# A three-level seven-for-eight product with its result transposed, in a kernel of layer norm, attention and a low-rank layer

## The chip, the cores and the metric

The kernel runs on one core of one Trainium2 chip. The metric is the time of one execution on the device in microseconds (us), median of three runs. A profile of one execution comes with it. The engines are named as the profile does: PE multiplies matrices and reads its weights through PEld, DVE, ACT and POOL compute on vectors, SP issues transfers (DMA). SBUF is the memory beside the engines, PSUM the one that PE writes its products to, in eight banks; DRAM is the memory outside.

## The reference

All values are 32-bit floats. `x` has the shape (4, 512, 1024): four batches of 512 tokens.

```python
xn = _layernorm(x, axis=-1)
qkv = hidden_states @ w_qkv                      # of xn: 32 heads of 128, 8 shared k and v heads
scores = jnp.einsum('bqhgd,bkhd->bhgqk', q, k) * scale
bias = -slopes[:, :, None, None] * sqrt_dist     # -inf above the diagonal
attn = jax.nn.softmax(scores + bias[None], axis=-1)
out = jnp.einsum('bhgqk,bkhd->bqhgd', attn, v).reshape(B, S, NH * D)
return out @ w_o
...
out = jnp.einsum('bsd,od->bso', hidden_states, W) + b      # of xn
lora_outputs = jnp.stack([x @ A[:r, :].T @ B[:, :r].T for r in RANKS], axis=1)
# one of the four ranks 8, 16, 32, 64 is chosen per token by a gate
...
x = x + _L0_attn_ref(xn, ...) + _L0_ffn_ref(xn, ...)
```

The two products that end in the result, `out @ w_o` over 4096 attention columns and `xn @ W.T` over 1024, have the same rows and columns. So the kernel computes one product: 2048 tokens by a contraction of 5120 by 1024 columns, and adds the low-rank term and `x`.

## The kernel before

**Seven products for eight.** A product of two matrices cut in quarters can be made with seven products of quarters. With the quarters a11 to a22 of the left matrix and b11 to b22 of the right one, `sums_a` (L142) forms s1 = a21 + a22, s2 = s1 - a11, s3 = a11 - a21, s4 = a12 - s2, and `sums_b` (L149) t1 = b12 - b11, t2 = b22 - t1, t3 = b22 - b12, t4 = b21 - t2. The products, by number, are a11·b11, a12·b21, s4·b22, a22·t4, s1·t1, s2·t2 and s3·t3 (`operand_a`, `operand_b`). The class `Inner` (L162) runs the seven in the order m1, m5, m4 of the item before, m6, m3, m2, m7, adds several into the same PSUM bank where it can, and has DVE or ACT read a bank out after each step: `read` (L173) by ACT if nothing is to be added to it and by DVE if there is, `last` (L182) always by DVE. A step's bank is used again by a step soon after, so a late read delays PE. A matmul of 32-bit floats is two instructions on PE.

**Stages.** PE's instructions keep the order of the program. On the other engines a scheduler sets the order, except where a call is wrapped in `pin`. The stages follow each other and overlap a little at their borders.

1. `project()` (L357) normalises `x`, transposes it and computes q, k and v with two levels of seven for eight: `sets` of columns for each pair p of batches, items i of the outer level in the order `PROJECTED`, and the seven inner steps of each by `Inner`. POOL makes the inner sums of the weights (`inner_w`, L504), DVE the outer ones (`outer_w`, L489) and the inner ones of the tokens (`Pair.inner`, L462). Work beside the steps stands in the queues `soon`, `later` and `weights`; `beside()` (L578) takes a piece of each after every step, of `later` only after every eighth (`pace[1]`). `put_by` (L443) stores the outer sums of the normalised tokens for the last product.
2. `attend()` (L765) runs over 32 units (p, h, bi): pair, shared head, batch in the pair. The scores of the next unit are made between the steps of the present one. For a row i of 128 tokens, PE makes four score tiles in three banks (L819), DVE adds the bias and finds the maximum (L824), ACT takes the exponential (L828), DVE inverts the sum (L831), POOL scales (L833), PE transposes (L844), DVE and ACT by turns copy the transposed tile to SBUF (`pt`, L847 and L849), PE multiplies with v (L857) and ACT copies the result into the tile `o` (L858). After the second batch of a head `put_by(p, h)` (L860) makes the four outer sums of the two batches' results on POOL (in `os`) and stores seven operands in 14 transfers of 256 KB on SP's queue; for the last head DVE makes the sums and ACT's queue takes the stores. `outer_weights()` (L875) goes on beside: 20 pieces of the weights are loaded, POOL makes four subtractions of 128 x 512 in each, and four sums are stored.
3. `finish()` (L1026) computes the last product with two levels: `order` (L950) has 2·7·2 = 28 items (p, i, kb): pair of batches, outer product, half of the contraction. `Operands` (L952) loads the four quarters of tokens (`sa`, L979) and of weights (`sw`, L971 to L976), 640 KB each. DVE makes the four token sums of an item and POOL the four weight sums, each on a tile of 128 x 1280 (`first_sums`, `sums`). A step is 5 x 2 matmuls with 128 tokens as PE's weights and 256 columns moving (L1016). The results of outer products stay in SBUF, in five tiles `r8` of 2048 values per partition, are summed there by `take_over` (POOL) and `after`, and leave from there (`store`, L1131). `x` comes in as the start value of each result quarter (`given`). The low-rank term is two more matmuls in four steps of four items (L1157).

Tokens' outer sums pass from stages 1 and 2 to stage 3 through DRAM (`s_d`), those of the weights from stage 2 (`t_d`). The tiles of the first item are loaded late in attention (`bring`), its first two sums are made there too (`add_up`), and its steps m1 and m5 are run among attention's last steps (`begin`, banks `begun`). These lines set it:

```python
order = [(p, i, kb) for p in range(NP) for i in OUTER for kb in range(2)]
...
for i in (3, 2, 1, 0):
    if nxt:
        scores(nxt, i)
    if i < 2:
        weigh(u, i + 2)
...
    transpose_probs(u, i)
...
weigh(u, 1)
...
weigh(u, 0)
...
if u[2] == 1:
    put_by(u[0], u[1])
```

Of the kernel before, what the change touches and what calls it, by code (L numbers as in the profile page):

```python
# [18 lines left out]
P = 128  # L19
# [34 lines left out]


@with_exitstack
def kernel(
# [35 lines left out]
    stats = ctx.enter_context(tc.tile_pool(name="stats", bufs=2))  # L93
# [19 lines left out]
    ag = const.tile([P, NC, RMAX + NR], F32, tag="ag", name="ag")  # L113
    gb = const.tile([P, NR], F32, tag="gb", name="gb")


    def scratch(name, shape):
# [7 lines left out]
    s_d = {  # L125
        (p, i, kb): scratch(f"s{p}_{i}_{kb}", [P, 2, 2, KB, HS])
        for p in range(NP) for i in OUTER for kb in range(2)
    }
    t_d = {(i, kb): scratch(f"t{i}_{kb}", [P, 2, 2, KB, HS]) for i in (4, 5, 6, 7) for kb in range(2)}

    def by_quarters(d, kp, src, queue=nc.sync):

        for e in range(2):
            queue.dma_start(out=d[:, :, e, kp, :], in_=src[:, e, :].rearrange("p (r k) -> p r k", r=2))
# [27 lines left out]
    class Inner:  # L162
# [10 lines left out]
        def read(self, dst, src, row, col):  # L173
            if self.base is None:
                if self.begun is None:
                    nc.scalar.copy(dst, src)  # L176
                else:
                    nc.vector.tensor_copy(dst, src)
            else:
                add(nc.vector, dst, src, self.base(row, col))  # L180
# [10 lines left out]
        def first(self, which, m):  # L191
            if self.begun is not None:
                return self.begun[which]
            bank = self.bank(which, self.name)
            self.mult(m, bank, True)
            return bank
# [20 lines left out]
        def m2(self):  # L217
            a = self.bank("a", self.name)
            self.mult(2, a, True)
            self.last(0, 0, a, self.t1)  # L220
# [65 lines left out]

    us = {}
# [69 lines left out]
    def project():  # L357
        with pool("a") as sb:
# [60 lines left out]
            class Pair:  # L419
# [3 lines left out]
                def __init__(self, p, homes):  # L423
                    self.p, self.homes, self.X, self.XO, self.XI = p, homes, {}, {}, {}
# [18 lines left out]
                def put_by(self, i):  # L443
                    for c in range(2):
                        by_quarters(s_d[self.p, i, 0], c, self.XO[i][:, c::2, :])
# [16 lines left out]
                def inner(self, i, eng):  # L462
# [4 lines left out]
                    t = buf(f"xi{i}", f"xi{i}_{self.p}")  # L467
# [185 lines left out]

            def once(f, *args):
# [7 lines left out]
            def hand_over(a, b, i):  # L662
# [15 lines left out]
                else:  # L678
                    soon.append(once(b.home, 3))
                    for j in (3, 7, 4, 5):  # L680
                        if j in (3, 7):
                            soon.append(b.outer(j, (V, V, V, V)))
                        soon.append(once(b.put_by, j))
                        soon.append(b.inner(j, V))
                    soon.extend(once(b.put_by, j) for j in (1, 2, 6))

            def stream():
# [28 lines left out]
                for st in sets[:2]:  # L716
                    for i in (1, 2):
                        need(a, i)
                        yield item(st, i, accs[st])
                        if st == sets[0] and i == 1:  # L720
                            for j in (1, 2):
                                soon.append(once(a.put_by, j))
# [9 lines left out]
                for j in (3, 7, 4, 5):  # L732
                    if j in (3, 7):
                        soon.append(a.outer(j, (V, V, V, V)))
                    soon.append(once(a.put_by, j))
                    soon.append(a.inner(j, GP if j == 4 else V))
                soon.append(once(a.put_by, 6))
# [27 lines left out]
    def attend(front, begin):  # L765


        with pool("b") as sb:
            bank = rotation(sc=(0, 1, 2), tr=(3, 6, 7), o=(4, 5))
            units = [(p, h, bi) for p in range(NP) for h in range(NKV) for bi in range(2)]  # L770
            sizes = {"wr": (2, DOUT), "wsum": (2, S), "q": (G, S), "k": (S,), "vT": (S,), "bias": (G, S)}
            counts = {"q": 2, "k": 2, "vT": 2, "v": 2, "pt": 10, "o": 3}
# [3 lines left out]
            sizes.update(v=(NT, D), pt=(S,), os=(3, 2, S), o=(G, S))  # L776
# [83 lines left out]
            def put_by(p, h):  # L860

                o = [O.pop((p, h, bi)) for bi in range(2)]
                a = [o[r][:, 2 * j : 2 * j + 2, :] for r in range(2) for j in range(2)]
                t = buf("os", f"os_{p}_{h}")
                s = [t[:, 0], t[:, 1], a[2], t[:, 2]]
                end = (p, h) == (NP - 1, NKV - 1)
                sums_a(nc.vector if end else nc.gpsimd, *s, *a)
                kb, kp = divmod(h + 2, KB)
                for i in OUTER:
                    by_quarters(  # L870
                        s_d[p, i, kb], kp, operand_a(i, a[0], a[1], a[3], s),
                        nc.scalar if end else nc.sync,
                    )

            def outer_weights():  # L875

                for kb in range(2):
                    for kp in range(KB):
                        for e in range(2):
                            n = f"{kb}_{kp}_{e}"  # L880
                            w = buf("wr", f"wr_{n}")
                            pin(nc.sync.dma_start(
                                out=w, in_=rows_of(kb * KB + kp, slice(0, DOUT))[:, :, e]
                            ))
                            yield
                            b11, b12, b21, b22 = [w[:, k, ts(j, S)] for k in range(2) for j in range(2)]
                            t = buf("wsum", f"wsum_{n}")
                            pin(sub(nc.gpsimd, t[:, 0], b12, b11))
                            pin(sub(nc.gpsimd, t[:, 1], b22, t[:, 0]))
                            pin(sub(nc.gpsimd, b12, b22, b12))  # L890
                            pin(sub(nc.gpsimd, b21, b21, t[:, 1]))
                            for i, v in ((5, t[:, 0]), (6, t[:, 1]), (7, b12), (4, b21)):
                                nc.sync.dma_start(
                                    out=t_d[i, kb][:, :, e, kp, :],
                                    in_=v.rearrange("p (r k) -> p r k", r=2),
                                )
                            yield
# [335 lines left out]
```

## Time and profile before

| | |
|---|---|
| median of 3 runs | 2765.87 us (2763.76 to 2769.19) |
| the profiled execution | 2767.64 us |
| its span | 2765.8 us |
| mean clock granted to PE | 0.989 of full speed |
| instructions | 34769 |
| transfers | 450.6 MB, 163 GB/s over the span |
| score tiles, L819 (PE) / L824 (DVE) | x1024, 441 ns / x512, 490 ns |
| exponentials L828 (ACT) / scalings L833 (POOL) | x512, 554 ns / x512, 537 ns |
| transposes L844 / products with v L857 (PE) | x1280, 275 ns / x640, 592 ns |
| `s<-o`, `s<-os` (stores of attention) | x120 and x90, 256 KB each, 2.8 and 2.6 us to landing |
| `sa<-s`, `sw<-t` (loads of the last product) | x112 and x64, 640 KB each, 6.2 and 4.1 us to landing |

The times are one execution's, by the hardware profiler. "x1024, 441 ns" is a count and the mean time of one. Tile names stand left and right of an arrow: what is written, from what is read. Matmuls overlap, so the time of one is longer than the distance to the next. The projections last until about 1132 us after the span's start, attention until about 1873 us, the last product until the end. Where rows of a stage are compared, they come from the stretches 50 to 900, 1190 to 1850 and 1850 to 2766 us.

### The profile page before, as it was taken

To read this page: it belongs to the slowest core of one execution; us is meant where nothing else is said; L and a number is where in the kernel's file an instruction comes from. 1 tells how busy PE (TensorE), PEld (TensorE's weight loads), DVE (VectorE), ACT (ScalarE), POOL (GpSimd) and SP (SyncE) were. 2 spreads that over 40 slices of the span, in tenths; PEclk is the share of its full clock that TensorE was granted. 3 is DMA by queue.
4 is the path that set the end of the run, shared out by engine and by line. 5 is a ranking of instruction groups with operands and counts; after the bars stand their busy time and mean duration, and the time that the engine had idled before them with its cause. 6 is when DMAs were issued, how large, how long until landed. Compare 5 with 4: busy or idle time off the path is not lost.

```text
span 2765.8 us, 34769 instructions
## 1 busy us (share of the span) xinstructions
PE 2687.0 (97%) x12224; PEld 2158.9 (78%) x12224; DVE 1417.7 (51%) x3093; ACT 628.4 (23%) x1671; POOL 1579.2 (57%) x1670
## 2 busy tenths in 40 slices
PE   7899999989999999899999999997999999999999
PEld 6788888878888888566666666656888888888887
DVE  7655656576565555455555555554333442334432
ACT  3011111000000000566666666650000000000000
POOL 4565656666766666468787775654435433534531
PEclk9999999999999999999999999998999999999999
DMA  6333332263223221457676764627566556656551
GB/s 225 118 115 122 119 119 98 103 232 111 92 100 114 92 99 54 143 193 261 223 257 225 255 229 160 221 88 253 176 196 201 170 195 201 189 177 190 175 185 40
DMA packets 250400, 450.59 MB, mean 163 GB/s; under 512 B 17193, under 2 KB 164649, under 8 KB 246130
## 3 DMA queue, kind: packets, MB, share of 16 engines
q1 hardware_dynamic: 245554, 441.55, 47.5%
q10 hardware_dynamic: 4672, 6.82, 0.7%
q8 instruction: 97, 1.59, 0.2%
q14 instruction: 77, 0.63, 0.1%
HBM read 290.49 MB, written 157.82 MB: 162 GB/s over the span
## 4 chain that ended last, share of the span: by engine, by line
PE 91%; DVE 6%; DMA 2%; issue 1%; ACT 0%; POOL 0%; ACTq 0%; DVEq 0%; POOLq 0%
PE pc L1016 17%; PE pc_q L525 13%; PE po L857 10%; PE psc L819 10%; PE pd L1016 8%; PE pd_q L525 7%; PE pc_kv L525 6%; PE pa L1016 4%; PE ptr L844 4%; PE pa_q L525 3%; PE pd_kv L525 3%; PE pa_kv L525 2%; DVE pt L847 1%; DVE p L824 1%; PE pc_begun L1016 1%
## 5 line engine op out<-in xcount | busy, mean ns | idle before, releaser
L833 POOL TENSOR_SCALAR p<-p,tot 128x256 f32<-128x256 f32 (+3 forms) x512 | 262.9, 537 | 161.0 <-DVE tot L831 120.6
L140 POOL TENSOR_TENSOR t<-sw,sw 128x1280 f32<-128x1280 f32 x28 | 82.1, 2931 | 448.9 <-DMA sw<-t 260.9
L824 DVE CUSTOM_DVE_ANT_0 p<-psc,bias 128x256 f32<-128x256 f32 (+3 forms) x512 | 243.5, 490 | 156.7 <-PE psc L819 109.2
L819 PE MATMUL psc<-k,q 128*128 128x512 f32 (+3 forms) x1024 | 309.9, 441 | 12.3 <-DMA q<-q 6.6
L828 ACT ACTIVATE p<-p,low 128x256 f32<-128x256 f32 (+3 forms) x512 | 283.4, 554 | 84.3 <-DVE low L824 80.8
L857 PE MATMUL po<-pt,v 128*128 128x512 f32 x640 | 290.6, 592 | 0.0
L819 PEld LDWEIGHTS psc<-k,q 128*128 128x128 f32 x1024 | 173.3, 192 | 115.3 <-issue 60.6
L1016 PE MATMUL pc<-sw,sa 128*128 128x256 f32 x1080 | 237.7, 379 | 0.0
L1016 PEld LDWEIGHTS pc<-sw,sa 128*128 128x128 f32 x1080 | 205.2, 190 | 27.9
L844 PEld LDWEIGHTS ptr<-ident,p 128*128 128x128 f32 x1280 | 148.4, 141 | 70.9 <-POOL p L833 26.1
L847 DVE COPY pt<-ptr 128x512 f32<-128x512 f32 x192 | 130.2, 684 | 139.7 <-PE ptr L844 139.3
L857 PEld LDWEIGHTS po<-pt,v 128*128 128x128 f32 x640 | 116.8, 190 | 108.5 <-issue 99.2
L525 PE MATMUL pc_q<-xi,ti_q 128*128 128x256 f32 x704 | 182.1, 381 | 3.7 <-DVE q L137 2.4
L140 POOL TENSOR_TENSOR ti_q<-to_q 128x256 f32<-128x256 f32 x128 | 97.7, 783 | 136.2 <-PE pc_q L525 136.2
L844 PE MATMUL ptr<-ident,p 128*128 128x128 f32 x1280 | 168.6, 275 | 4.1 <-DVE pt L847 2.7
L525 PE MATMUL pc_q<-x,ti_q 128*128 128x256 f32 x640 | 165.4, 381 | 3.8 <-DVE r_q L137 2.5
L140 POOL TENSOR_TENSOR t<-sw,t 128x1280 f32<-128x1280 f32 x56 | 163.3, 2916 | 9.3 <-issue 4.4
L176 ACT COPY m<-pc 128x512 f32<-128x512 f32 x6 | 3.5, 587 | 702.7 <-PE pc L1016 702.7
L525 PEld LDWEIGHTS pc_q<-xi,ti_q 128*128 128x128 f32 x704 | 133.8, 191 | 23.0 <-DVE q L137 2.8
L525 PEld LDWEIGHTS pc_q<-x,ti_q 128*128 128x128 f32 x640 | 120.3, 191 | 23.4 <-DVE r_q L137 2.6
L140 POOL TENSOR_TENSOR ti_q<-w_q 128x256 f32<-128x256 f32 x96 | 68.8, 738 | 117.6 <-PE pc_kv L525 57.3
L1016 PE MATMUL pa<-sw,sa 128*128 128x256 f32 x560 | 125.5, 379 | 0.0
(251 smaller groups left out, 5272.4 us busy)
## 6 DMA issues: line engine op xcount, KB each, us to landing
sa<-s SPq DMA_DIRECT2D x112, 640.0 KB, 6.2
sw<-t SPq DMA_DIRECT2D x64, 640.0 KB, 4.1
w_q<-in_w_qkv_dram SPq DMA_DIRECT2D x16, 2048.0 KB, 8.9
q<-q SPq DMA_DIRECT2D x30, 1024.0 KB, 7.1
s<-o SPq DMA_DIRECT2D x120, 256.0 KB, 2.8
s<-os SPq DMA_DIRECT2D x90, 256.0 KB, 2.6
w_kv<-in_w_qkv_dram SPq DMA_DIRECT2D x16, 1024.0 KB, 5.6
q<-c_q SPq DMA_DIRECT2D x32, 512.0 KB, 2.6
```

The costliest lines, as they stand in the source:

```text
L140: return eng.tensor_tensor(dst, u, v, ALU.subtract)
L176: nc.scalar.copy(dst, src)
L525: nc.tensor.matmul(dst, ops_w[m][:, c, :], XI[i][m][:, c, :], start=start and c == 0, stop=c == 1, skip_group_check=True,)
L819: nc.tensor.matmul(sc[:, :n], Q[u][:, g, ts(i, P)], K[u][:, :n], start=True, stop=True)
L824: nc.vector.tensor_tensor_reduce(pr[:, g], sc[:, :n], bias[p, h][:, g, S - n :], -SCALE, BIG, ALU.add, ALU.min, low,)
L828: nc.scalar.activation(pr[:, g], pr[:, g], AF.Exp, bias=low, scale=-1.0, accum_out=tot[:, g : g + 1])
L833: nc.gpsimd.tensor_scalar(pr[:, g], pr[:, g], tot[:, g : g + 1], 1.0, ALU.mult, ALU.mult)
L844: nc.tensor.transpose(tr[:, ts(g, P)], PR[u, i][:, g, ts(j, P)], ident)
L847: nc.vector.tensor_copy(pt, tr)
L857: nc.tensor.matmul(po, V[u][:, j, :], PT[i, j], start=(j == 0), stop=(j == i))
L1016: nc.tensor.matmul(bk[:, t, :], s[:, k, ts(t, P)], w[:, k, :], start=start and k == 0 and t == 0, stop=k == KB - 1, skip_group_check=True,)
```

## The change

The last product gets a third level, the name `MIDDLE` in the code: each of the seven outer products is made with seven middle ones, and each of those with seven inner ones. That is 49 items (i, m) for 28. An item has 7 inner steps of 5 matmuls; weights (128 columns) stand in PE, and 256 tokens move. The outer rows are the two batches of a pair and the middle rows the two halves of their tokens, as the outer and inner ones were before; the inner rows are now the two pairs of batches, and the inner contraction its two halves (kb), over both of which the code looped before. As columns now stand in PE, the product comes out transposed: 128 PE transposes (four into one bank) and 32 DVE additions of `x` from PSUM turn it back before it is stored (`leave`, `turn`).

- **Token sums of two levels** are made and stored ahead. In attention `put_by` becomes `outer_sums` (the same four on POOL) and `middle_sums`: for each head 12 sums on DVE, eight of 128 x 512 and four of 128 x 768 elements, one taken by `aside()` at each of eight places in a unit. A head's seven stored operands of 2 x 256 KB in 14 transfers become 49 blocks of 128 KB in 18 transfers, all on SP's queue. In the projections `put_by` stores the inner sums that are there already.
- **The weights' outer sums** move from attention to the second half of the projections (`weights_put_by`): 40 pieces with two subtractions of 128 x 256 on POOL and two on DVE, taken from `later`, from which a piece is now taken after every third step (`pace[1] = 3`).
- **The weights' middle sums** are made in the last product on POOL, 8 halves of 128 x 1280 for each outer product (`Weights.sum`). Each item's inner sums are four of 128 x 1280 on DVE (tokens) and four of 128 x 640 on POOL (weights), in the order that `beside(n, slot)` writes out: all of these, and the loads, are pinned.
- **Results of outer products** no longer fit in SBUF together. They go to DRAM as `c_d` and come back as the start values of others (`KEPT`, `BASE`, `taken`).
- A reading with nothing to add now always goes to ACT. Of the first item m1 and m2 instead of m1 and m5 are run in attention; tiles of the statistics and of the gate move to the projections' pool; `o` has four buffers instead of three, `ot` is new with two.

The diff at its core:

```diff
+MIDDLE = (1, 2, 3, 6, 7, 4, 5)
+SLOT = {1: 0, 7: 1, 2: 2, 4: 3, 5: 4, 6: 5, 3: 6}
+SUMMED = {5: 0, 6: 1, 7: 2, 4: 3}
...
+            def weights_put_by(kp, e, j):
...
+                sub(nc.gpsimd, t[:, 0], b12, b11)
+                sub(nc.gpsimd, t[:, 1], b22, t[:, 0])
+                yield
+                sub(nc.vector, b12, b22, b12)
+                sub(nc.vector, b21, b21, t[:, 1])
+                d = t_d[:, :, j, e, kp]
+                nc.sync.dma_start(out=d[:, 0:2], in_=t)
+                nc.sync.dma_start(out=d[:, 2:4], in_=w.rearrange("p a b k -> p (a b) k")[:, 1:3])
...
+                    for j in OUTER:
+                        later.append(b.put_by(j))
+                    for kp in range(2 * KB):
+                        for e in range(2):
+                            for j in range(2):
+                                later.append(weights_put_by(kp, e, j))
+                    pace[1] = 3
...
+            def middle_sums(p, h, which, of, t, kept):
...
+                eng = nc.gpsimd if (p, h) == last and of == "o" and not kept else nc.vector
+                pin(add(eng, s1, a21, a22))
+                yield
+                pin(sub(eng, s2, s1, a11))
+                yield
+                pin(sub(eng, s4, a12, s2))
+                yield
+                pin(sub(eng, s3, a11, a21))
...
+                        nc.sync.dma_start(out=d[:, :4], in_=a[:, k].rearrange("p e r k -> p (e r) k"))
+                    nc.sync.dma_start(out=d[:, 4:], in_=m[:, :3, k])
...
+                if bi == 1:
+                    beside.append(middle_sums(p, h, (1, 2), "o", O[p, h, 0], True))
...
                 for i in (3, 2, 1, 0):
                     if nxt:
                         scores(nxt, i)
+                    aside()
                     if i < 2:
                         weigh(u, i + 2)
                         next(fill, None)
                     transpose_probs(u, i)
+                    aside()
...
+                if bi == 1:
+                    o, t = outer_sums(p, h)
+                    beside.append(pause(1))
+                    beside.append(middle_sums(p, h, (7, 4), "o", o, False))
+                    beside.append(middle_sums(p, h, (5, 6, 3), "os", t, False))
...
-    order = [(p, i, kb) for p in range(NP) for i in OUTER for kb in range(2)]
+    order = [(i, m) for i in OUTER for m in MIDDLE]
...
+        def sum(self, m, half):
...
+            r = slice(half * KB, (half + 1) * KB)
+            pin(sub(nc.gpsimd, q[dst][:, r], q[u][:, r], q[v][:, r]))
...
+        def load(self, r, f):
...
+            pin(nc.sync.dma_start(out=t, in_=s_d[self.i][:, SLOT[self.m], r, f]))
+
+        def tokens(self, k):
...
+                pin(add(nc.vector, s[1], a[1, 0], a[1, 1]))
...
+        def weights(self, k):
...
+            pin(sub(nc.gpsimd, t[k], u, v))
...
+            for k in range(KB):
+                nc.tensor.matmul(
+                    bk, w[:, k], x[:, k], start=start and k == 0, stop=k == KB - 1,
+                    skip_group_check=True,
+                )
...
+                        nc.tensor.transpose(tr[:, k, j], t[:, j, p, ts(k, P)], ident)
+                y = x_t[:, p].rearrange("p a (b k) -> p a b k", b=2)
+                pin(add(nc.vector, y, tr, y))
+                nc.sync.dma_start(out=rows(outf, p, *where), in_=x_t[:, p])
...
+            if slot == 1:
+                if nxt:
+                    nxt.quarters(W[nxt.i])
+                    nxt.tokens(1)
+                    nxt.weights(1)
+            elif slot == 2:
+                bring(n + 2, 0, 0)
+                if nxt:
+                    nxt.tokens(2)
+                    nxt.weights(2)
+            elif slot == 3:
+                bring(n + 2, 1, 1)
+                if nxt:
+                    nxt.weights(3)
...
+            elif slot == 4:
+                if nxt:
+                    nxt.tokens(4)
+                    nxt.weights(4)
+            elif slot == 5:
+                if nxt:
+                    nxt.tokens(3)
+                if k < 4:
+                    W[i].sum((5, 6, 7, 4)[k], 0)
+            elif slot == 6:
+                bring(n + 2, 0, 1)
+                if k < 4:
+                    W[i].sum((5, 6, 7, 4)[k], 1)
+            elif slot == 7:
+                bring(n + 2, 1, 0)
+            if leaving and slot >= 5:
+                leaving.popleft()()
```

Here `k` is the item's place among the seven of its outer product, and slot 1 follows m1, slot 2 m5, slot 3 the m4 of the item before, slots 4 to 7 m6, m3, m2 and m7.

## The prediction

> **What bounds it now.** I read the busy shares and slices first, then the busy time by stretch, then the groups of instructions, then single stretches of the timeline.
>
> ```profile
> PE 2687.0 (97%) x12224; PEld 2158.9 (78%) x12224; DVE 1417.7 (51%) x3093; ACT 628.4 (23%) x1671; POOL 1579.2 (57%) x1670
> ...
> PE   7899999989999999899999999997999999999999
> ...
> POOL 4565656666766666468787775654435433534531
> ```
>
> The matmul engine is at nine tenths in all slices but a few: any wait given to it is lost, and any matmul taken away is gained, in every stage. The stretches (busy us with counts, for PE, PEld, DVE, ACT, POOL; then clock, DMA share, GB/s) are the projections, attention and the last product:
>
> ```profile
> 50.00:900.00 850.00, 827.93 (x3909) 723.23 (x3908) 530.66 (x1107) 85.54 (x199) 536.60 (x673) 0.99 0.35 122
> ...
> 1190.00:1850.00 660.00, 650.65 (x2748) 397.05 (x2747) 354.25 (x1208) 443.06 (x1233) 479.19 (x601) 1.00 0.63 216
> 1850.00:2766.00 916.00, 893.85 (x4121) 780.15 (x4119) 337.76 (x321) 13.49 (x23) 374.86 (x139) 0.99 0.56 178
> ```
>
> The groups give durations (mean ns of one), and the last two show that an equal add on DVE takes 1.5 or 2.0 us:
>
> ```profile
> L1016 PE MATMUL pc<-sw,sa 128*128 128x256 f32 x1080 | 237.7, 379 | 0.0
> L140 POOL TENSOR_TENSOR t<-sw,t 128x1280 f32<-128x1280 f32 x56 | 163.3, 2916 | 9.3 <-issue 4.4 <-POOL sw L140 1.7 <-DMA sw<-in_w_o_dram 0.8
> ...
> L140 DVE TENSOR_TENSOR s<-sa,s 128x1280 f32<-128x1280 f32 x28 | 42.0, 1500 | 0.0
> ...
> L137 DVE TENSOR_TENSOR s<-sa,sa 128x1280 f32<-128x1280 f32 x28 | 56.6, 2023 | 100.5 <-DMA sa<-s 100.4
> ```
>
> **The row that decides.** Late in attention the kernel puts two such adds on DVE while POOL adds too (timeline: start, us, engine, what, idle before):
>
> ```profile
> 1800.22 2.89 POOL L140 TENSOR_TENSOR t<-sw,sw 128x1280 f32<-128x1280 f32 x1
> ...
> 1800.98 3.48 DVE L137 TENSOR_TENSOR s<-sa,sa 128x1280 f32<-128x1280 f32 x1
> ...
> 1803.19 4.01 POOL L140 TENSOR_TENSOR sw<-sw,sw 128x1280 f32<-128x1280 f32 x1
> ...
> 1804.50 4.05 DVE L140 TENSOR_TENSOR sa<-sa,sa 128x1280 f32<-128x1280 f32 x1
> 1808.47 0.68 DVE L824 CUSTOM_DVE_ANT_0 p<-psc,bias 128x512 f32<-128x512 f32 x1
> ...
> 1809.21 1.13 PE L819 MATMUL psc<-k,q 128*128 128x512 f32 x2 [3.73 <-DVE low L824]
> ```
>
> The DVE add waits for the end of POOL's, POOL's next for the end of DVE's. They take turns and never overlap; the reads of the scores wait behind, and PE loses 3.73 us. Reads of PSUM on DVE keep 0.68 to 0.69 us beside busy POOL. The Trainium skill says this in "SBUF — State Buffer", "SBUF: two separate sides": DVE operations with two SBUF inputs and POOL share one port pair under an exclusive lock for the whole instruction. It speaks against this change, which adds such work on both engines where PE gets less. With the lock the two sums are added, without it the larger one counts; I work out both.
>
> **Last product, PE.** Matmuls 2·7·2·70 = 1960 become 7·7·35 = 1715. Each is two instructions; 20 of them start 4.32 us apart (1910.78 to 1915.09), 0.2158 us each. Gain 245·2·0.2158 = 105.8. Low-rank matmuls stay 64. Added: 128 transposes. L844's mean is 275 ns, as "TensorE: Matmul & The Clock Gate", Part 4, also says of transposes in one kernel (35 us in all), but 16 of them take 1.88 us from start to start, 0.108 each: 13.9. Net -91.9 if PE stays the bound.
>
> After attention's last matmul (1873.1) 892.7 us remain: 4020 instructions (867.7), a wait, a slow restart and the tail:
>
> ```profile
> 1890.95 7.04 PE L1016 MATMUL pc_begun<-t,s 128*128 128x256 f32 x20 [15.25 <-DVE m L178]
> ```
>
> **Does that wait go?** The first items no longer need the last head, but the third inner product needs s2. Ahead of it on DVE stand four outer sums (1.23 each) and four of 768 elements (0.87 by interpolation), taking turns with POOL's four sums (1.24) and three weight sums. s2 comes some 17 us after attention, PE needs it after 3.5: about 14 stay (0 to 18). So PE alone would give 14 + 3544·0.2158 + 13.9 + 5.5 of tail = 798, 94 less.
>
> **Last product, DVE and POOL.** Counted in the changed program's instruction order:
> - DVE adds of 1280: 195 at 1.40 (starts of the undisturbed ones) = 273. Of 256: 28 at 0.33 (interpolated between 512 and 1280) = 9. Last head: 8.
> - POOL: 195 of 640. No row has this size; 256 takes 0.70, 512 1.24, 1280 2.855 between starts, so 1.51: 294. Sums of 1280: 56·2.855 = 160. Adds of 256: 116·0.70 = 81. 8 of 1024 at 2.37 = 19. Last head 5, low-rank columns 9.
> - POOL 568, DVE 290, together 858 under the lock, against 779 for PE. Before it was about 375 + 170 of 893: harmless.
>
> By the lock rule the stage takes 0.8 + 858 + 4, plus time in which both stand still. That occurs where PE is behind: middle products 7 and 4 hold 11.6 and 14.4 us of DVE and POOL work beside 15.1 of PE (up to 28 over seven outer products), and while the first loads of item 1, queued on SP behind the last head's stores, arrive (5). I take 20: 883, a gain of only 9. DVE's other 311 reads (about 0.42, or 0.69 for the 32 turned blocks) run beside POOL. Each s1 also waits on DVE for a load issued at the preceding item's end (L979 lands in 6.2); behind it stand the reads of PSUM, due 4.3 us after their matmul, two steps. I count it in the 20.
>
> DMA: 200 MB in this stage instead of 160. At 178 GB/s for a share of 0.56, full use is about 318 GB/s, 630 us: not the bound. SP issues (0.3 to 0.6 each) also have room. The reads between steps are halves of the old size; ACT takes 64 of them.
>
> **Attention.** POOL loses 80 weight sums of 1.27 (102 us, off the path). DVE gains 192 sums of heads, 0.60 (512) or 0.87 (768): 133 us. Stores per head rise from 14 of 256 KB to 49 blocks of 128 KB in 18 issues, while the weights' DMAs leave: bytes stay equal. PE is dense here and DVE has no margin early in a unit:
>
> ```profile
> 1532.24 1.28 DVE L847 COPY pt<-ptr 128x512 f32<-128x512 f32 x2
> ...
> 1532.98 0.66 PE L844 MATMUL ptr<-ident,p 128*128 128x128 f32 x4 [0.19 <-DVE pt L847]
> ```
>
> PE's fourth score of a row waits for the bank of its first (three banks). In that order, per head:
> - Unit with the head's second batch: two sums of 768 before the reads of row 2, with one POOL scaling (0.68) between: 2.42, less DVE's gap of 0.7 and 0.4 of margin = 1.3 on PE. A sum before row 1: 0.4. One before row 0: 0.5.
> - Next unit: the first sum of products 7 and 4 waits for POOL's outer sum (2.37 each, ending about 10.4 into the unit), the second for a scaling: the reads of row 1 come 1.7 late, 1.45 on PE; before row 0 0.7.
>
> 4.35 per head, 15 heads: +65. Ends: 20 if no sum waits for POOL (0.6 to 0.9 per unit), 100 if each waits for a whole operation (1 us more per unit).
>
> **Projection.** 40 units of two POOL and two DVE subtractions of 256 come beside the second half. POOL waits there on PE for buffers (L140 ti_q, 136 us in one group), which covers its 40·1.4. DVE's pair is 2·(0.33 + 0.7 of lock) = 2.06 where a read is due in two steps of 0.86 less 0.42; some 0.35 per unit is lost: +14 (0 to 40). The pair also waits for POOL's sums and their loads, with PSUM reads behind; that is its upper end. put_by there only issues DMAs (share 0.35).
>
> **Sum.** 2765.8 + 65 + 14 - 9 = 2836. The profiled execution took 2767.64, 1.8 around the span and 1.8 over the median 2765.87, so the sum stands for the median as it is.
>
> **Rivals.**
> - *Faster, the port is not the bound of the product* (0.20): if POOL's 640 cost under 1.2 us, or its idle places fit DVE's adds, so that the sum falls to 779, PE decides: -94, with 20 in attention and 5 in projection 2765.8 - 94 + 25 = 2697. For it: DVE and POOL were half idle. Against: 1800 to 1808 shows strict turns.
> - *Milder* (0.20): the lock holds in the product, sums in attention find gaps: +20 + 5 - 9 = 2782.
> - *Heavier* (0.12): idle of 40 in the product (+11), attention +100, projection +30: 2907.
> - The change not doing what it says: the counts above exclude it.
>
> Forecast case 0.48, 2805 to 2870. Range 2740 to 2900: part of the faster and of the heavier case is left out. About 0.2% (5.5 us) cannot be told from none. Faster 0.22, same 0.03, slower 0.75.
>
> **Right or wrong.** Right: in the product DVE adds of 1280 average well over 1.5 us, POOL is busy nearly throughout, PE waits on t and s; in attention PE waits on low and pt, some 2 us a unit. Wrong: the product as dense as now, ending about 800 us after attention, or attention still 22.9 us a unit.

## The result and the profile after

The changed kernel takes **2933.15 us**, median of 4 runs (2932.93 to 2941.27), against 2764.85 (2763.76 to 2769.19) for the kernel before, run beside it: a ratio of 1.0613, 95% interval 1.0591 to 1.0634. The forecast was 2836 with a range of 2740 to 2900. The direction was right, the size was not: 168 us for 70.

The page of the changed kernel, with the same rows as before (busy shares, then 40 slices of 73 us):

```profile
PE 2673.0 (91%) x11862; PEld 2108.6 (72%) x11862; DVE 1841.8 (63%) x3584; ACT 644.5 (22%) x1723; POOL 2001.6 (68%) x1922
...
PE   7999999997888899999999999996889899898979
...
POOL 4566565676676666556566666663969899897776
PEclk9999999999999999999999999997999999999989
DMA  7333332475656531345656565747777676675764
```

PE has fewer instructions (11862 for 12224) and is busy less, but the span is 166 us longer. PE's row shows where: a seven and four eights in slices 10 to 14, in the projections, where there had been nines; a six for a seven where the last product begins; and eights and a seven from there to the end.

I divide each profile at the starts of the projections' last matmul (L525, now L535) and attention's last product with v (L857, now L886 or L887 with an experiment's extra lines):

| us, from the profiles | projections end | attention | last product | span |
|---|---|---|---|---|
| before | 1118.9 | 753.6 | 893.3 | 2765.8 |
| changed | 1215.0 | 792.8 | 923.7 | 2931.5 |
| difference | +96.1 | +39.2 | +30.4 | +165.7 |
| forecast | +14 | +65 | -9 | +70 |

So of the 96 us by which the span misses the forecast, 82 are in the projections, a stage in which the change only put 160 subtractions with their loads and stores, and 39 in the product; attention gives 26 back.

**Projections.** Busy time in the stretch 650 to 1050 us, first of the kernel before (length, then busy us and counts of PE, PEld, DVE, ACT, POOL, then clock, DMA share, GB/s), then of the changed one:

```profile
650.00:1050.00 400.00, 400.00 (x1855) 351.50 (x1854) 233.49 (x464) 28.78 (x78) 268.53 (x347) 1.00 0.27 99
```

```profile
650.00:1050.00 400.00, 337.18 (x1418) 283.05 (x1417) 215.98 (x435) 22.33 (x60) 271.02 (x344) 0.93 0.56 179
```

PE never stood still before. Now it makes 1418 matmuls for 1855. At the old pace of 400/1855 these would take 306 us, so 94 us are lost: 63 idle and 31 in longer busy time. The mean granted clock of 0.93 accounts for about 28 of these 31 (0.07 of 400 us). No other engine is busier to speak of: POOL 2.5 us longer, DVE and ACT less. The longest waits of PE and of DVE in that stretch (waiting group, awaited group, us in total, times, longest):

```profile
PE pc_q L535 <- DVE u_q L137: 26.1, 8, 5.7
...
DVE wr L140 <- POOL wsum L140: 83.7, 58, 5.2
DVE q L137 <- PE pc_q L535: 23.1, 29, 3.2
```

All waits of PE there end at a reading of PSUM by DVE. The DVE pair of each piece of weights waits 2.1 us on average for POOL's pair (83.7 us over 40 pieces), and the timeline shows how this reaches PE (start, us, engine, what, idle before):

```profile
857.37 0.72 POOL L140 TENSOR_TENSOR wsum<-wr 128x256 f32<-128x256 f32 x1 [3.67 <-DMA wr<-in_w_o_dram]
...
858.13 0.42 DVE L140 TENSOR_TENSOR wr<-wr 128x256 f32<-128x256 f32 x1 [1.81 <-POOL wsum L140]
...
859.17 0.93 DVE L140 TENSOR_TENSOR wr<-wr,wsum 128x256 f32<-128x256 f32 x1 [0.62 <-POOL wsum L140]
860.02 0.41 DVE L137 TENSOR_TENSOR u_q<-pc_q,u_q 128x256 f32<-128x256 f32 x1
860.36 0.41 DVE L137 TENSOR_TENSOR q<-pc_q,u_q 128x256 f32<-128x256 f32 x1
...
860.82 1.13 PE L535 MATMUL pc_q<-x,ti_q 128*128 128x256 f32 x4 [1.51 <-DVE q L137]
```

POOL waits for a load, DVE's pair for POOL, two readings of PSUM stand behind the pair, and PE waits for the second of them. Elsewhere POOL's pair is late because it stands behind inner sums of weights whose buffers PE still reads, so that the three wait in a ring: in this stretch POOL waits 25 us for such loads and 83 us for PE.

**Last product.** DVE's waits from 2009 us on, and the durations of the token sums on DVE and of the inner weight sums on POOL (count, busy us, mean ns, idle before):

```profile
DVE s L137 <- DMA sa<-s: 140.3, 40, 10.6
DVE m L137 <- PE pc L1094: 37.8, 23, 3.9
...
DVE s L137 <- DMA sa11y<-s: 8.7, 1, 8.7
```

```profile
L140 DVE TENSOR_TENSOR s<-sa,s 128x1280 f32<-128x1280 f32 x49 | 116.0, 2368 | 0.0
```

```profile
L140 POOL TENSOR_TENSOR t<-w,t 128x640 f32<-128x640 f32 x84 | 177.2, 2109 | 13.3 <-PE pc L1094 10.0
```

The adds do take turns: 2.37 us where one undisturbed took about 1.49. But DVE also stands 149 us at s1, waiting for loads. How this reaches PE is seen at the longest of three places where the transposes wait for POOL's sums `v` of outer products, 23.2 us together, PE's largest group of waits in this stage:

```profile
2691.22 1.49 DVE L137 TENSOR_TENSOR s<-sa,sa11z 128x1280 f32<-128x1280 f32 x1 [8.39 <-DMA sa<-s]
...
2694.15 0.42 DVE L137 TENSOR_TENSOR x<-pc,u 128x256 f32<-128x256 f32 x1
...
2698.13 3.58 POOL L137 TENSOR_TENSOR v<-v,x 128x1024 f32<-128x1024 f32 x1
...
2701.77 1.12 PE L1184 MATMUL ptr_f<-ident,v 128*128 128x128 f32 x4 [9.40 <-POOL v L137]
```

DVE's readings `x` stand behind s1, POOL's sums behind the readings, and the transposes behind POOL. In all, PE is idle for 103 us of the stage, and busy for 820 us with what takes 779 at the old pace (3544 instructions at 0.2158 us, and the transposes); the mean granted clock is 0.94 there, 0.99 before.

### The profile page after: what moved, and what is told of

It reads as the page before. It is cut to its first block, busy times and chain, and to the rows that moved or that the text cites. A ratio compares the mean times of both kernels' runs of the same rounds, so it can differ in the third digit from the quotient of the medians.

```text
span 2931.5 us, 35510 instructions
## 1 busy us (share of the span) xinstructions
PE 2673.0 (91%) x11862; PEld 2108.6 (72%) x11862; DVE 1841.8 (63%) x3584; ACT 644.5 (22%) x1723; POOL 2001.6 (68%) x1922
## 4 chain that ended last, share of the span: by engine, by line
PE 36%; DVE 9%; POOL 8%; issue 6%; DMA 5%; ACT 1%; SPq 1%; DVEq 0%; POOLq 0%; ACTq 0%
PE po L886 8%; PE pc L1094 8%; PE psc L848 5%; PE pd L1094 4%; DMA sa<-s 3%; PE pc_q L535 3%; PE pa L1094 2%; POOL t L140 2%; DVE pt L876 2%; PE ptr L873 2%; PE pd_q L535 1%; DVE ot L140 1%; DVE p L853 1%; ACT p L857 1%; POOL o L140 1%
## 5 line engine op out<-in xcount | busy, mean ns | idle before, releaser
L862 POOL TENSOR_SCALAR p<-p,tot 128x256 f32<-128x256 f32 (+3 forms) x512 | 333.0, 668 | 242.6 <-DVE tot L860 125.5
L848 PE MATMUL psc<-k,q 128*128 128x512 f32 (+3 forms) x1024 | 317.6, 443 | 46.0 <-DVE low L853 39.3
L857 ACT ACTIVATE p<-p,low 128x256 f32<-128x256 f32 (+3 forms) x512 | 283.4, 554 | 137.9 <-DVE low L853 133.6
L886 PE MATMUL po<-pt,v 128*128 128x512 f32 x640 | 290.6, 592 | 0.0
L535 PE MATMUL pc_q<-x,ti_q 128*128 128x256 f32 x640 | 173.6, 395 | 46.9 <-DVE u_q L137 26.4
L140 POOL TENSOR_TENSOR t<-w 128x640 f32<-128x640 f32 x84 | 173.0, 2060 | 37.1 <-DMA w<-in_w_o_dram 30.1
L535 PE MATMUL pc_q<-xi,ti_q 128*128 128x256 f32 x704 | 188.9, 392 | 9.9 <-DVE q L137 9.7
L886 PEld LDWEIGHTS po<-pt,v 128*128 128x128 f32 x640 | 116.8, 190 | 108.5 <-issue 99.2
L140 POOL TENSOR_TENSOR t<-w,t 128x640 f32<-128x640 f32 x84 | 177.2, 2109 | 13.3 <-PE pc L1094 10.0
L535 PEld LDWEIGHTS pc_q<-x,ti_q 128*128 128x128 f32 x640 | 122.2, 196 | 73.6 <-DVE u_q L137 30.4
L535 PEld LDWEIGHTS pc_q<-xi,ti_q 128*128 128x128 f32 x704 | 137.6, 197 | 32.4 <-DVE q L137 12.0
L175 ACT COPY m<-pc 128x256 f32<-128x256 f32 x30 | 11.2, 372 | 612.1 <-PE pc L1094 448.5
L175 ACT COPY q<-pc_q 128x256 f32<-128x256 f32 x64 | 23.8, 372 | 460.2 <-PE pc_q L535 460.1
L1094 PE MATMUL pd<-s,t 128*128 128x256 f32 x490 | 118.8, 391 | 6.5 <-DVE s L137 4.3
L535 PE MATMUL pd_q<-xi,ti_q 128*128 128x256 f32 x448 | 117.0, 384 | 2.8 <-POOL ti_q L140 2.8
```

Source lines behind the costliest of these rows:

```text
L140: return eng.tensor_tensor(dst, u, v, ALU.subtract)
L535: nc.tensor.matmul(dst, ops_w[m][:, c, :], XI[i][m][:, c, :], start=start and c == 0, stop=c == 1, skip_group_check=True,)
L848: nc.tensor.matmul(sc[:, :n], Q[u][:, g, ts(i, P)], K[u][:, :n], start=True, stop=True)
L857: nc.scalar.activation(pr[:, g], pr[:, g], AF.Exp, bias=low, scale=-1.0, accum_out=tot[:, g : g + 1])
L862: nc.gpsimd.tensor_scalar(pr[:, g], pr[:, g], tot[:, g : g + 1], 1.0, ALU.mult, ALU.mult)
L886: nc.tensor.matmul(po, V[u][:, j, :], PT[i, j], start=(j == 0), stop=(j == i))
```

## The experiments

The kernels are compared stage by stage, since an edit in one stage leaves the other two nearly as they were: over the runs in which a stage was not touched, attention varies by 4 us, the product by 7 and the projections by 9. The exception is no_mid, whose edit also takes away the last head's sums, for which PE waits at the start of the product.

| run | projections end | attention | product | time, median | ratio to before, 95% |
|---|---|---|---|---|---|
| w_pool | 1184.6 | 793.2 | 930.4 | 2908.56 | 1.0506 to 1.0538 |
| w_dve | 1167.5 | 796.5 | 929.4 | 2892.3 | 1.0442 to 1.0477 |
| early | 1217.8 | 793.3 | 926.1 | 2937.51 | 1.0601 to 1.0638 |
| early_late | 1132.6 | 794.8 | 882.6 | 2810.37 | 1.0150 to 1.0184 |
| tok_late | 1205.7 | 792.4 | 882.9 | 2885.1 | 1.0419 to 1.0453 |
| no_wsum | 1206.6 | 793.1 | 905.2 | 2909.27 | 1.0511 to 1.0547 |
| both | 1208.1 | 792.3 | 861.9 | 2866.76 | 1.0356 to 1.0387 |
| no_tsum | 1210.5 | 792.7 | 830.3 | 2836.39 | 1.0249 to 1.0280 |
| no_mid | 1214.7 | 745.0 | 914.0 | 2874.46 | 1.0383 to 1.0415 |
| best | 1136.7 | 743.0 | 887.9 | 2765.71 | 0.9987 to 1.0004 |
| best2 | 1133.3 | 742.7 | 894.1 | 2769.43 | 1.0012 to 1.0032 |
| best4 | 1133.6 | 741.9 | 886.0 | 2767.67 | 1.0001 to 1.0014 |

### Projections: the pair of subtractions and its loads

**w_pool**

```diff
-                sub(nc.vector, b12, b22, b12)
-                sub(nc.vector, b21, b21, t[:, 1])
+                sub(nc.gpsimd, b12, b22, b12)
+                sub(nc.gpsimd, b21, b21, t[:, 1])
```

> The changed kernel with the weights' two DVE subtractions of each piece in the projections put on POOL, behind the two that POOL already makes. In the changed kernel the projections' last matmul starts at 1214 us (1118 before). Theory (DVE waits in its order for POOL's sums, 84 us in 58 waits, and the readings of PSUM stand behind): these waits are gone, the projections end at 1120 to 1145, the whole takes 2835 to 2865. Rival 1 (the new loads and stores of this stretch, DMA share 0.57 for 0.27, slow it): the projections end after 1195, the whole stays over 2910. Rival 2 (POOL is short of time there: 80 more subtractions of 0.7 us delay the inner sums of the weights): 1150 to 1190, 2870 to 2910.

The end came at 1184.6: 30 us gained, and 66 still lost. That is what the second rival gave, but POOL's waits from 650 to 1190 us show that it was not short of work time alone:

```profile
POOL wsum L140 <- DMA wr<-in_w_o_dram: 25.1, 13, 4.6
POOL ti_q L140 <- PE pc_q L535: 21.5, 8, 3.1
POOL wsum L140 <- issue: 21.4, 8, 4.2
POOL wsum L140 <- DMA wr<-in_wt_dram: 14.7, 6, 3.2
```

It stood 61 us for the pieces' loads or their issue, with the inner sums that PE needs behind. PE now waits for these directly, where it waited for DVE's readings before:

```profile
PE pd_q L535 <- POOL ti_q L140: 22.6, 11, 2.9
```

**w_dve**

```diff
-                sub(nc.gpsimd, t[:, 0], b12, b11)
-                sub(nc.gpsimd, t[:, 1], b22, t[:, 0])
+                sub(nc.vector, t[:, 0], b12, b11)
+                sub(nc.vector, t[:, 1], b22, t[:, 0])
```

> The changed kernel with all four of the weights' subtractions of each piece in the projections on DVE: twice the DVE work of this kind, but no wait for POOL. Theory (the wait for POOL's sums is the cost): the projections end at 1130 to 1170 instead of 1214, since DVE waits for loads only; the whole takes 2845 to 2890. Rival (it is the two-input work on DVE beside POOL that costs, by their taking turns): the doubled work costs more, the projections end at 1214 or later and the whole takes 2930 or more.

Twice the DVE work, and the projections end 47 us earlier, inside the band of the theory: the wait between the engines costs more than the work and the turns at the port. What is left here is in part the loads, for which DVE now waits 25 us. The whole lies 2 us over its band.

**early**: loads one place of the queue earlier, pair left on DVE.

```diff
                     nc.sync.dma_start(out=w[:, :, c], in_=rows_of(kp, ds(c * S + j * HS, HS))[:, :, e])
+                yield
                 yield
                 t = r4(f"wsum_{kp}_{e}_{j}")[:, 0].rearrange("p (b k) -> p b k", b=2)
```

> The changed kernel with one edit in the projections: the loads of a piece of weights are issued one place of the queue (three steps) further ahead of its subtractions; two of these stay on DVE. Of the two by two, three are measured: loads as they were, pair on DVE: projections end at 1206 to 1215 us; loads as they were, pair on POOL: 1184.6; loads earlier, pair on POOL: 1132.6. If the late loads are the root of DVE's waits for POOL's sums: 1135 to 1160, the whole 2850 to 2875. If DVE waits because POOL itself is held up by its other sums: 1180 or later, the whole 2895 or more.

Nothing gained. POOL hardly waits for loads any more (12 us), but for PE, and DVE for POOL, as before. From 650 to 1150 us, DVE and POOL:

```profile
DVE wr L140 <- POOL wsum L140: 90.6, 61, 5.5
...
POOL ti_q L140 <- PE pc_q L535: 84.0, 31, 4.8
POOL ti_kv L140 <- PE pc_kv L535: 28.1, 11, 3.7
```

**early_late** has w_pool's edit, the earlier loads, and the later token sums of tok_late below.

> The changed kernel with three edits that keep its result: the weights' subtractions in the projections all on POOL, their loads one place of the queue (three steps) further ahead of them, and the token sums of the last product one or two steps later. With the subtractions on POOL alone the projections ended at 1184.6 us, with the later sums alone the product took 883 us. Theory (what was left in the projections is POOL's wait for these loads, 40 us, and for their issue, 21): the projections end at 1145 to 1168, the whole takes 2815 to 2850. Rival (POOL is at 0.84 there and has no room left): they end at 1178 or later, the whole takes 2855 or more.

The two edits in the projections together end them at 1132.6, better than expected and 14 us behind the kernel before; where these 14 come from was not tried. The same stretch as above:

```profile
650.00:1050.00 400.00, 390.35 (x1798) 340.19 (x1797) 223.51 (x450) 28.28 (x76) 356.26 (x472) 1.00 0.59 191
```

PE is at full clock again with a DMA share of 0.59, higher than in the changed kernel, so traffic by itself was not the cause. The four corners are: neither 1206 to 1215, loads 1218, pair 1185, both 1133. The pair on DVE closes the ring; the late loads matter once it is open.

### Attention

**no_mid** leaves out the twelve sums of each head on DVE; the stores keep number and size.

```diff
...
-                pin(add(eng, s1, a21, a22))
                 yield
-                pin(sub(eng, s2, s1, a11))
                 yield
-                pin(sub(eng, s4, a12, s2))
                 yield
-                pin(sub(eng, s3, a11, a21))
...
-                    nc.sync.dma_start(out=d[:, 4:], in_=m[:, :3, k])
+                    nc.sync.dma_start(out=d[:, 4:], in_=a[:, k].rearrange("p e r k -> p (e r) k")[:, :3])
```

> The changed kernel without the twelve two-level token sums per head on DVE in attention, whose stores stay as many and as large (they store parts that are there). From the projections' last matmul to attention's last it takes 793 us (754 before). Theory (DVE's sums stand ahead of the readings of the scores and of pt): 750 to 762, the whole 2890 to 2905. Rival (the 18 stores per head and their traffic): 780 or more, the whole over 2915.

Attention takes 745.0: the sums cost 47.8, some 3 us a head, and the stores nothing that shows. It is 8.6 shorter than before the change, when POOL also made the weights' sums in this stage. Stage and whole are below their bands; the whole also because the product is 10 us shorter: with the last head's sums gone, PE's wait for s2 at its start falls from 13.9 to 3.7 us. How the sums reach PE, in the timeline of early_late, whose attention is that of the changed kernel:

```profile
1503.54 0.68 DVE L140 TENSOR_TENSOR ot<-ot,o 128x512 f32<-128x512 f32 x1
1504.14 0.41 DVE L854 CUSTOM_DVE_ANT_0 p<-psc,bias 128x256 f32<-128x256 f32 x1
...
1504.62 0.70 PE L849 MATMUL psc<-k,q 128*128 128x256 f32 x2 [1.21 <-DVE low L854]
...
1505.15 3.60 PE L887 MATMUL po<-pt,v 128*128 128x512 f32 x8
1505.35 0.42 DVE L854 CUSTOM_DVE_ANT_0 p<-psc,bias 128x256 f32<-128x256 f32 x1
1506.86 0.91 DVE L140 TENSOR_TENSOR ot<-o,ot 128x512 f32<-128x512 f32 x1
```

A sum stands just ahead of the readings of the scores, and PE's fourth score tile waits 1.21 us for the first one's bank. Right after it PE is occupied for 3.6 us with the products with v, and once the readings are done, DVE's only long piece of work in that time is one sum of 0.91 us. The version below puts the sums there.

### The last product

**tok_late** issues each token sum one or two steps later.

```diff
             if slot == 1:
...
-                    nxt.tokens(1)
...
             elif slot == 2:
...
-                    nxt.tokens(2)
...
             elif slot == 3:
...
+                    nxt.tokens(1)
...
             elif slot == 4:
                 if nxt:
-                    nxt.tokens(4)
+                    nxt.tokens(2)
...
             elif slot == 5:
                 if nxt:
-                    nxt.tokens(3)
+                    nxt.tokens(4)
...
             elif slot == 6:
                 bring(n + 2, 0, 1)
+                if nxt:
+                    nxt.tokens(3)
```

> The changed kernel with the four token sums of an item on DVE in the last product issued one or two steps later (s1 after m4, s2 after m6, s4 after m3, s3 after m2), their loads as before. The last product takes 924 us from attention's last matmul (894 before). Theory A (DVE waits at s1 for loads, 149 us in 41 waits, with readings of PSUM behind): these waits fall below 40 us and the product takes 850 to 890, the whole 2860 to 2900. Theory B (DVE and POOL take turns, and their sum is the bound): the adds of 1280 keep about 2.3 us, the product stays at 900 or more, the whole at 2910 or more.

41 us gained by order alone. DVE's waits for `sa` fall to 18.4 us, while its adds even rise to 2.5 us. The transposes' wait for POOL falls with them, from 23.2 us:

```profile
PE ptr_f L1184 <- POOL v L137: 6.3, 3, 4.3
```

**no_wsum** and **both** leave out the inner weight sums on POOL; both has the later token sums too.

```diff
...
-            pin(sub(nc.gpsimd, t[k], u, v))
+            t[k] = {1: b[0, 1], 2: b[1, 1], 3: b[0, 1], 4: b[1, 0]}[k]
```

> The changed kernel without the inner sums of the weights on POOL in the last product (196 of 128 x 640; the matmuls read the quarters themselves, so the result is another one). Theory B (DVE and POOL take turns): DVE's adds of 1280 fall from 2.36 us to under 1.7, the product from 924 to 800 to 845, the whole to 2810 to 2855. Theory A (DVE's waits for token loads): these 149 us stay, the product takes 880 or more, the whole 2890 or more.

> The changed kernel with the token sums of the last product later, and without the inner sums of the weights on POOL (the matmuls read the quarters themselves). Later sums alone: product 883 us; inner sums away alone: 905; neither: 924. Theory A and B together (a wait for loads and the turns of DVE and POOL, each enough to hold PE up): product 800 to 835, more than the two gains added (865), DVE's adds of 1280 under 2.0 us; the whole 2800 to 2840. Rival A alone (loads were all, turns cost nothing): product 870 or more, the whole 2865 or more.

196 sums less on POOL, busy 349 us for 765, bring 18 us, and 21 with the later token sums. That is theory A for the greater part; for both it fits neither band, since 862 is 8 us better than A alone and 27 worse than A and B. The two gains simply add up (41 and 18, together 62).

**no_tsum** leaves out the token sums on DVE.

```diff
...
-                pin(add(nc.vector, s[1], a[1, 0], a[1, 1]))
...
-                pin(sub(nc.vector, s[3], a[0, 0], a[1, 0]))
+            s[k] = {1: a[1, 0], 2: a[0, 1], 4: a[0, 1], 3: a[1, 0]}[k]
```

> The changed kernel without the token sums on DVE in the last product (the matmuls read the loaded quarters themselves); POOL keeps its sums. Theory A and B: POOL's adds of 640 fall from 2.08 to about 1.55 us, DVE's readings no longer stand behind waits for loads, PE decides: product 800 to 840, the whole 2805 to 2850. Rival (the loads themselves come too late for PE, or the weights' sums on POOL are the bound): product over 870, the whole over 2880.

The product takes 830.3. With DVE's adds gone, POOL's are undisturbed:

```profile
L140 POOL TENSOR_TENSOR t<-w,t 128x640 f32<-128x640 f32 x84 | 129.9, 1546 | 49.1 <-PE pc L1083 45.8
```

So the turns at the port are real (1.55 us alone, 2.11 in turns), and DVE's sums cost 93 us in the product, of which a later order alone wins back 41.

What remains at 830 over PE's own 779 us is mostly the start. The first 120 us of the product, of the changed kernel and of no_tsum:

```profile
2007.80:2127.80 120.00, 88.18 (x346) 73.10 (x345) 84.12 (x59) 3.47 (x9) 93.86 (x43) 0.82 0.72 229
```

```profile
2003.20:2123.20 120.00, 96.56 (x414) 82.37 (x413) 27.57 (x41) 3.84 (x10) 82.59 (x49) 0.87 0.83 266
```

At 0.2158 us each, 120 us hold 556 PE instructions. The changed kernel loses 210 of them, 45 us, no_tsum 142, 31 us; the kernel before, with 473 in its first 120 us, lost 18. Three things follow each other there: the wait for s2 behind the last head's sums, a slow restart, and the second item's weights, whose loads stand on SP behind the last head's stores. That the last head's sums make the first wait is shown by no_mid. PE in early_late:

```profile
1945.71 4.61 PE L1095 MATMUL pc_begun<-s,t 128*128 128x256 f32 x10 [14.14 <-DVE s L140]
...
1963.09 2.07 PE L1095 MATMUL pc<-sa,w 128*128 128x256 f32 x4 [8.39 <-DMA w<-in_wt_dram]
```

### A version with all that was found

**best** adds to early_late: sums in attention behind the products with v, a seventh tile `r4` (with the low-rank columns loaded by halves, to make room), and another order of the first loads.

```diff
                     if i < 2:
                         weigh(u, i + 2)
+                        aside()
+                        aside()
...
                 weigh(u, 0)
+                aside()
+                aside()
```

> A version with the result kept: subtractions on POOL and earlier loads in the projections, later token sums in the product (these together 2810 us), and besides: the sums of attention are issued after the products with v, two at a time, instead of just behind the scores; seven tiles r4 for six in the product (PE lost 20 us at one place where DVE waited 17.8 us for the store of one of them), with the low-rank columns loaded by halves to make room; and the weights of the second item loaded before three of its token quarters. Theory: attention 752 to 772 us for 795, product 845 to 868 for 883, the whole 2735 to 2775. Rival (the sums hold up the copies pt instead, and the tile was not what DVE waited for): attention 785 or more, product 878 or more, the whole 2795 or more.

Attention falls from 794.8 to 743.0, better than expected, with the same twelve sums: PE's waits for `low` (36 us in 650 of early_late) are gone. The product gains nothing (887.9, in the rival's band), although PE's waits for `r`, which the seventh tile was to end, fell from 8.4 to 1.0 us. In it, PE now waited 13.1 us at one place for POOL's last sums of outer product 7, in front of the transposes.

**best2** makes that sum first and the transposes later:

```diff
+                    pin(add(nc.gpsimd, v, v, t))
+                    if not leaving:
+                        leaving.extend([lambda: None] * 3)
+                    leave(v, (1, 1, r, c))
                     pin(add(nc.gpsimd, y, y, t))
                     pin(nc.sync.dma_start(out=c_d["y", r, c], in_=y))
-                    pin(add(nc.gpsimd, v, v, t))
-                    leave(v, (1, 1, r, c))
```

> The last version (2765.7 us: projections to 1136.7, attention 743.0, product 887.9) with one edit in the product: at the end of the outer product that is left with two results, POOL first makes the sum that is to be turned, and the transposes of it are put three places later in PE's order, where PE had waited 13.1 us for POOL. Theory: product 866 to 878, the whole 2742 to 2757, faster than the kernel before. Rival (POOL is behind there anyway, and PE waits for its inner sums t next): product 883 or more, the whole 2760 or more.

**best4** is best2 with the last head's sums all on DVE (`eng = nc.vector`).

> The same with the last head's sums all on DVE (four of them had been on POOL, in turns with DVE's). PE's wait of 13.1 us at the border of attention and product: by the turns of DVE and POOL it falls to 9 to 11 us, the whole 2 to 5 us under the version sent with it; if DVE's own work is what counts, no change within 2 us.

Both miss: best2 is in the rival's band, and best4 is 1.8 us under it, where 2 to 5 were expected, though its wait at the start fell further than expected. The waits aimed at went: 13.1 us at the turn, and at the start 11.4 to 6.2. Others came: PE's waits for DVE's readings `m` rose from 8.0 to 12.1 and 16.3, those for `r` from 1.0 to 8.5 and 9.5. The product stays at 886 to 894. Measured against the kernel before, best is the same (0.9996), best4 and best2 are 0.1% and 0.2% slower. No version beat it.

## Why the prediction was wrong

**Projections, the step that failed.** It priced the pair at "2·(0.33 + 0.7 of lock)" and "some 0.35 per unit", and it took POOL's waits for PE as cover ("which covers its 40·1.4"). The wait of DVE's pair for POOL's sums was named, but bounded with everything else at 40. Measured: 96, with 84 us of waits of DVE's pair for POOL. The cover was the fault: because POOL waits there for PE, everything that waits for POOL waits for PE too, and here that was DVE, for whose readings PE waits. By early and w_dve, neither the loads nor the work nor the port carried it alone; with the ring opened by w_pool's edit, the earlier loads bring another 52 us. Nearly a third of the loss (28 of 94 in the stretch shown) came on top through the clock, which the forecast had not priced at all.

**Attention: right mechanism, size too large.** 4.35 per head was forecast; the sums cost 47.8 over 16 heads by no_mid, 3.0 each. A second term was missing with the other sign: without the sums attention is 8.6 shorter than it was, and what had left it is POOL's weight sums, counted as "off the path". That they were the cause was not tried by itself. Together this makes +39 instead of +65. PE waits on `low` as said, 39 us in all for 4 before, which is 1.2 us a unit and not some 2; on `pt` hardly more than before (4 us for 3).

**Product: a term of the sum mis-sized, and the bound named wrongly.** "I take 20" was the term for the times when both stand still, with the waits at s1 in it. These waits alone cost 41 by tok_late. The transposes were priced at their own 13.9 us, and their wait for POOL's sums, 23.2 us, at nothing; 17 of it are among the 41. With the waits at s1 gone, the product takes 883, the very number that was forecast from 858 under the lock. But this agreement is luck and does not confirm that sum: by it, taking 196·1.55 = 303 us of POOL's work away should have left PE's 798, and both measured 862. The turns are real, and are not what sets the stage. PE's own floor was too low: 798 was forecast, no_tsum gives 830. About half of the difference is the start, priced at 14 us in this floor (and 5 for loads in the 20); it cost 31 even there, 45 in the changed kernel. The wait of 14 itself came as forecast (13.9); the slow matmuls behind it and the loads of the second item's weights came on top.

What sets the rest of the product between 830 and 883 is not settled: DVE and POOL each stand in many short waits there, and removing the largest ones moved the time to others.

**The marks.** DVE's adds well over 1.5 us: yes. POOL busy nearly throughout: 765 of 924 us, no. PE waiting on t and s: hardly (2 and 4 us after the start); it waits for readings of PSUM, and at the transposes for POOL's sums. Of the rivals, "the port is not the bound of the product" was right about the port and still wrong about the time. "Heavier" came nearest in number, at 2907, but by luck: its largest term was 100 in attention, where 39 came, and in the projections it had 30 for 96.

## What to carry to other kernels

Before an instruction with a new wait goes on an engine that also reads PSUM, follow the awaited engine's own queue: if that one waits for PE, the three form a ring, and the idle time that seemed to be cover becomes the cost. Place side work where the engine that needs the readings is occupied with something else: the same twelve sums per head cost 48 us ahead of the readings and nothing that shows behind PE's longest products. A sum of the work of two engines that take turns is a floor for a stage, not its time: start, loads and order come on top, and taking work away shows which of them decides.

## What was not expected of the hardware

A short wait can cost PE more than its length, and the length alone does not tell. In early_late, ten matmul instructions that take 2.32 us at full pace took 4.61 after the wait of 14.14 us, at a granted clock of 0.50, and after two short waits:

```profile
1987.50 4.08 PE L1095 MATMUL pd<-s,t 128*128 128x256 f32 x10 [2.12 <-DVE s L137]
...
2388.89 2.42 PE L1095 MATMUL pd<-s,t 128*128 128x256 f32 x10 [3.60 <-POOL t L140]
```

The granted clock was 0.58 in the first and 1.00 in the second, after the longer wait. In the stretch of the projections above, single waits were at most 5.7 us long, and the mean granted clock was 0.93.
